# Eight fetched experts per chunk and a shared last tile, in place of all sixteen experts for every token

## The chip, the cores and the metric

One Trainium2 chip, one of its cores. The metric is device microseconds of that core for one execution; lower is better. The engines are named as in the profile: PE (TensorE), DVE (VectorE), ACT (ScalarE), POOL (GpSimd), SP (SyncE, which here only issues DMAs).

## What is computed

The input `x` is 128 sequences of 64 tokens with 128 features; `ctx_1024` has the same shape. Everything is float32. Four residual steps follow each other:

```python
x = x + L0_xattn(layernorm(x), ctx)      # 16 heads of 8
x = x + L0_ffn(layernorm(x))             # 8 experts each pick 8 tokens of a sequence and attend among them
x = x + L1_xattn(layernorm(x), ctx)      # self-attention, cross-attention, a 128-512-128 net, three layernorms
x = x + L1_ffn(layernorm(x))             # the expert layer that the change is about
```

The expert layer has 16 routed experts and 2 shared ones, each with three 128 x 128 matrices:

```python
scores = sigmoid(x @ router_w.T);  s = scores + bias
keep the 2 best of 4 groups of experts, then the 4 best experts of those by s
w = 2.5 * scores[chosen] / sum(scores[chosen])          # combine weights, 0 for the other 12
h, u = x @ gate_w[e], x @ up_w[e]                       # for every e
routed = sum over e of w[e] * ((silu(h) * u) @ down_w[e])
y = routed + shared experts (weight 1)
```

The bias spreads by 0.8 between the experts, while the scores lie between 0 and 1, so that some experts are chosen by nearly every token and some by hardly any.

## The kernel before

The 8192 tokens are 16 chunks of 512 (8 sequences). A chunk's features lie over the 128 partitions and its tokens along the free axis when it is multiplied (`zT`), or tokens over partitions in four groups of 128 when it is normalized. Chunks 0 to 15 first go through the first layer (loop at the end of `two_layers`, with `routed_attention` for two chunks at a time); the results go to DRAM (`x_mid`). Then each chunk goes through `decoder_block` and `expert_layer`.

Nothing is issued when the Python code runs. The class `Plan` records every operation and gives it a cost in us by the function `duration` (for PE, 0.86 for a 128x512 matmul; for SP, 0.4 for the issue of a DMA and 2.2 and more until it has landed). `Plan.run` then simulates five engines with these costs and writes the instructions in the order in which they would start, at most `WINDOW` = 5 chunks past the oldest unfinished one, each engine strictly in order. So every recorded operation has the same line in the profile, L364 (the call in `Plan.run`), and it is told apart by its tile. Buffers are named slots: `PLACES` says which tags share them. SP issues nearly all DMAs, in one queue of instructions, in order; a DMA whose buffer or data is not ready holds up all that stand behind it.

The expert layer before:

- Six loads bring all 18 experts' matrices to SBUF once (`wg`, `wu`, `wd`), after the first layer has let go of these places.
- `run(c, x)` normalizes the chunk (`normed`, `turned`: `zT`) and calls `route`, which computes the combine weights `w` with some 40 small DVE instructions, transposes them (`psc`), copies them on DVE (`comb`), writes them to DRAM (`comb_d`), and reads them back by eight DMAs of two experts each, every row spread over all 128 partitions (`all_w`, 512 KB each).
- Then a loop over 18 experts, each on all 512 tokens. PE does `gate` and `up`, ACT a tanh (`mo_g`), DVE two steps (`mo_g`, `mo_a`: silu times up), POOL a multiplication by `all_w[e]` (routed experts only), and PE adds `wd[e]` times that to the sum `py`.
- `py` is copied (`yT`), transposed (`pt`) and added to `x`, which goes out.

In PSUM `gate` and `up` share five banks with other matmuls; `mo_g` and `mo_a` have three buffers each.

In `Attention.run`, used three times per chunk, the keys are spread by head in four copies (`kx`): two by ACT, two by DVE; the queries (`q`) are scaled on DVE.

Of the kernel before, what the change touches and what calls it, by code (L numbers as in the profile page):

```python
# [17 lines left out]
F32 = mybir.dt.float32  # L18
I32 = mybir.dt.int32
AF = mybir.ActivationFunctionType  # L20
ALU = mybir.AluOpType
# [17 lines left out]
NG, TKG, TOPK = 4, 2, 4  # L39
EPG = E1 // NG  # L40
BEHIND = 100
EARLY = 6
# [22 lines left out]

C_M4, C_BM, C_RK, C_COS, C_SIN, C_TRI, C_R8, C_END = 0, 4, 132, 134, 198, 262, 278, 286


# [94 lines left out]
class Plan:  # L163
# [3 lines left out]
    def __init__(self, tc, window, prompt=(), pace=0, places=None):  # L167


        self.prompt, self.pace, self.places, self.after = prompt, pace, places or {}, set()  # L170
        self.behind = 0.0
        self.tc, self.nc, self.window = tc, tc.nc, window
        self.ops, self.chunk, self.group = [], 0, None
        self.free, self.turns, self.known = {}, {}, {}
        nc = tc.nc
        self.V, self.A, self.G, self.T, self.Y = (
            Recorder(self, e, n) for e, n in ((nc.vector, "V"), (nc.scalar, "A"), (nc.gpsimd, "G"), (nc.tensor, "T"), (nc.sync, "Y"))
        )
# [190 lines left out]


class Recorder:
    def __init__(self, plan, eng, name):
# [6 lines left out]
def duration(engine, method, out, args, kw):  # L379

    n = elements(out)
    if engine == "T":
        if method == "transpose":
            return 0.11, 0.3, (128, False)
        lhsT, rhs = kw["lhsT"], kw["rhs"]
        k, m = (lhsT.shadow if isinstance(lhsT, View) else lhsT).shape[:2]
        one = max(0.00084 * n, 0.00087 * max(m, 64))
        together = (4 if k <= 32 else 2 if k <= 64 else 1) * (2 if m <= 64 else 1)
        return 2 * one / together, 0.3, (min(k, 64) if k <= 32 else 128, m <= 64)
    if engine == "Y":  # L390
        return 0.4, 2.2 + n * out.shadow.shape[0] * 5.0e-6 * 4, None
# [20 lines left out]
    "r": ["r.0", "r.1", "lg.0", "lg.1"], "h0": ["rot.0"], "h1": ["rot.1"],  # L412
    "z4": ["hotT1.0"], "zT4": ["zr.0", "zr.1"], "yT": ["hotT0.0"], "comb": ["zTr.0"],
    "mo_g": ["y.0", "ra_v.0", "ra_v.1"], "mo_a": ["scT.0", "rsc.0", "rsc.1"],
    "all_w": ["trig.0", "xp.0", "wvo.0", "sw.0", "sw.1"],
    "wg": ["xg.0"], "wu": ["xg.1"], "wd": ["wqk.0"],
    "m2": ["m.0", "m.1", "m.2"], "py": ["m.3"],
# [3 lines left out]
def two_layers(ctx: ExitStack, tc: tile.TileContext, a: dict, out: bass.AP):  # L421
# [8 lines left out]
    make_identity(nc, ident)  # L430
    cst = const.tile([P, C_END], F32, name="cst")
    nc.sync.dma_start(out=cst, in_=a["consts"])
# [16 lines left out]

    ones = const.tile([P, S], F32, name="ones")  # L450
    nc.vector.memset(ones, 1.0)
# [3 lines left out]


    x_mid = [kept.tile([P, T, P], F32, name=f"xm{c}", tag=f"xm{c}") for c in range(NCH)]

# [44 lines left out]
    class Attention:  # L503
# [10 lines left out]
        def __init__(self, pl, sb, ps, n_v, n_kx):  # L514
            one = const
            self.pl, self.sb, self.ps, self.n_kx = pl, sb, ps, n_kx

            v_bd = [one.tile([P, NB, NP, 2 * V1], F32, name=f"v_bd{i}", tag=f"v_bd{i}") for i in range(n_v)]
            self.v_bd = [pl.held(t) for t in v_bd]
            for t in self.v_bd:  # L520
                pl.G.memset(t, 0.0)
                pl.G.memset(t[:S, :, :, HD : HD + 1], 1.0)
                pl.G.memset(t[S:, :, :, V1 + HD : V1 + HD + 1], 1.0)

            self.bk = {}
            for w in ("L0_xattn_", "L1_xattn_sa_", "L1_xattn_ca_"):
                self.bk[w] = one.tile([P, NR], F32, name=f"bk{len(self.bk)}", tag=f"bk{len(self.bk)}")
                nc.vector.tensor_scalar(self.bk[w], cst[:, C_M4 : C_M4 + NR], col[w + "bk"], None, ALU.mult)
            self.n = 0

        def run(self, c, zT, kvT, w, resid, dst, mask=None, role="", bank="m"):
# [10 lines left out]
            for h in range(NR):  # L542
                place = cst[:, C_M4 + h : C_M4 + h + 1]
                if h < 2:
                    A.activation(kx[:, h], psk, AF.Identity, bias=self.bk[w][:, h : h + 1], scale=place)
                else:
                    V.tensor_scalar(kx[:, h], psk, bk, place, ALU.add, ALU.mult)
            psq = m([P, CH], "psq")
            T_.matmul(psq, lhsT=wq, rhs=zT, start=True, stop=True)
            q = pl.new(sb, [P, CH], "q", self.n_kx, tag="q" + role)  # L550
            V.tensor_scalar(q, psq, bq, 1.0 / math.sqrt(HD), ALU.add, ALU.mult)

# [103 lines left out]
    def routed_attention(pl, sb, ps, dram):  # L656
# [8 lines left out]

        big = lambda name, tag, slots: pl.new(sb, [P, (E1 + 2) * P], name, slots, tag=tag)
        wqk = big("wqk", "wqk", 1)[:, : 2 * E0 * P].rearrange("p (e f) -> p e f", e=E0)
# [72 lines left out]
        def run(c, xs):  # L740
# [41 lines left out]
            for half in range(2):  # L782
# [48 lines left out]
                with pl.one():  # L831
                    for t in range(4):
                        T_.matmul(psa[:, t], lhsT=v[:, t], rhs=scT[:, t], start=True, stop=True)
                V.tensor_copy(xp[:, :, part].rearrange("p q e r -> p e q r"), psa.rearrange("p e (q r) -> p e q r", r=KT))

            for i, (x, gated) in enumerate(zip(xs, gates)):
# [72 lines left out]
    def expert_layer(pl, sb, dram, ps):  # L909
# [4 lines left out]
        pl.Y.dma_start(out=bias, in_=a["L1_ffn_bias"].unsqueeze(0).to_broadcast([P, E1]))  # L914
        wg, wu, wd = (pl.new(sb, [P, (E1 + 2) * P], n).rearrange("p (e f) -> p e f", f=P) for n in ("wg", "wu", "wd"))
        loads = [
            (wg, a["L1_ffn_gate_w"].rearrange("e d f -> d e f"), a["L1_ffn_sh_gate_w"].rearrange("d (u f) -> d u f", u=2)),
            (wu, a["L1_ffn_up_w"].rearrange("e d f -> d e f"), a["L1_ffn_sh_up_w"].rearrange("d (u f) -> d u f", u=2)),
            (wd, a["L1_ffn_down_w"].rearrange("e f d -> f e d"), a["L1_ffn_sh_down_w"].rearrange("(u f) d -> f u d", u=2)),
        ]  # L920
        last = []
        for w, routed, shared in loads:
            for part, src in ((w[:, :E1], routed), (w[:, E1:], shared)):
                pl.Y.dma_start(out=part, in_=src)
                last.append(pl.ops[-1])
        tri = cst[:, C_TRI : C_TRI + NG * NG].rearrange("p (i j) -> p i j", i=NG)
# [15 lines left out]

        def route(z):

# [55 lines left out]
            comb = pl.new(sb, [E1, CH], "comb", 1)  # L1000
            V.tensor_copy(comb, psc)

            flat = pl.new(dram, [E1, CH], "comb_d", 2)
            pl.Y.dma_start(out=flat, in_=comb)
            all_w = []
            for i in range(0, E1, 2):
                t = pl.new(sb, [P, 2, CH], "all_w")
                pl.Y.dma_start(out=t, in_=flat[i : i + 2].unsqueeze(0).to_broadcast([P, 2, CH]))
                all_w += [t[:, k] for k in range(2)]
            return all_w  # L1010

        def run(c, x):
            pl.after = set(last)
            zT = turned(pl, normed(pl, x, sb, role="4", n=1), sb, ps, "m2", role="4")
            pl.after = set()
            all_w = route(zT)
            py = pl.new(ps, [P, CH], "py")
            for e in range(E1 + 2):
                ph = pl.new(ps, [P, CH], "gate", tag="me")
                T_.matmul(ph, lhsT=wg[:, e], rhs=zT, start=True, stop=True)  # L1020
                pu = pl.new(ps, [P, CH], "up", tag="me")
                T_.matmul(pu, lhsT=wu[:, e], rhs=zT, start=True, stop=True)

# [3 lines left out]
                act = pl.new(sb, [P, CH], "mo_a", in_turn=True)  # L1027
                if e < E1:
                    V.tensor_tensor(act, g, pu, ALU.mult)
                    G.tensor_tensor(act, act, all_w[e], ALU.mult)  # L1030
                else:
                    V.scalar_tensor_tensor(act, g, 0.5, pu, ALU.mult, ALU.mult)
                T_.matmul(py, lhsT=wd[:, e], rhs=act, start=e == 0, stop=e == E1 + 1)
            yT = pl.new(sb, [P, CH], "yT", 1)
# [5 lines left out]
            V.tensor_tensor(x, x, pt, ALU.add)  # L1040
            pl.Y.dma_start(out=pl.held(out[c]), in_=x)
        return run

# [19 lines left out]
    for c in range(NCH):  # L1063
# [8 lines left out]
        attend.run(c, zT, cT, "L0_xattn_", x, x)  # L1072
        if c == 1:
            the_rest(pl)
            routed = routed_attention(pl, sb, ps, dram)
        if c % 2:
            routed(c - 1, xs[c - 1 :])

    for c in range(NCH):
        pl.chunk = NCH + c  # L1080
        pl.behind = BEHIND
        if c == 0:
            decoder = decoder_block(pl, sb, ps, attend)
            pl.after = marks[-1]
            experts = expert_layer(pl, sb, dram, ps)
            pl.after = set()
        x, cT = loaded(c, pl.held(x_mid[c]))
        pl.after = marks[EARLY if c < 2 else NCH // 2 - 1] if c <= WINDOW else set()
        decoder(c, x, cT)
        pl.after = set()  # L1090
        experts(c, x)
    pl.run()


def _constants():

    import numpy as np

    c = np.zeros((P, C_END), np.float32)
    p = np.arange(P)  # L1100
# [10 lines left out]
    i = np.arange(NG)  # L1111
    c[:, C_R8:] = np.arange(1, KT + 1)
    c[:, C_TRI:C_R8] = (i[None, :] < i[:, None]).astype(np.float32).reshape(-1)
# [41 lines left out]
```

## Time and profile before

| | |
|---|---|
| median of 3 runs | 2013.98 us (2008.09 to 2018.83) |
| the profiled execution | 2008.47 us |
| its span in the trace | 2006.5 us |
| mean granted clock of PE | 0.974 |
| first expert matmul of the second layer (`gate`, `py`) | from about 680 us |
| first `out` issued | 780.2 us |
| last `out` issued | 2003.5 us |
| chunk to chunk in the steady part (`sc` on POOL at 1006.88, 1097.33, 1187.78 us) | 90.45 us |
| longest waits of SP | for DVE's `comb` 605.7 us, for DVE's `x` 539.3 us |

The profile shows one execution. An engine's busy time counts the time in which at least one of its instructions ran. A float32 matmul is two instructions on PE; they are pipelined, and the end of each is modelled, so the time of one is read from the distance between starts. Groups give the count, the summed busy time, the mean of one, and then the idle time just before them with what ended it. SP's DMA issues appear as SPq.

### The profile page before, as it was taken

How to read it: one execution, taken by the hardware profiler on the slowest of the kernel's cores; microseconds unless marked ns; L12 is line 12 of the kernel's file. 1: busy time of each engine (PE TensorE's matmuls, PEld its weight loads, DVE VectorE, ACT ScalarE, POOL GpSimd, SP SyncE). 2: the span in 40 equal slices, each digit the busy share in tenths (PEclk: the TensorE clock that was granted, in tenths of full speed). 3: DMA queues.
4: the chain of work that ended last, by engine and by line, in shares of the span. 5: the costliest groups of instructions: out<-in, count | busy, mean ns of one | idle time of the engine just before them, and what ended most of it. 6: DMA issues, size and time to landing. Idle time of an engine off the chain costs nothing.

```text
span 2006.5 us, 41482 instructions
## 1 busy us (share of the span) xinstructions
PE 1876.2 (94%) x16032; PEld 1176.9 (59%) x16032; DVE 1490.5 (74%) x3694; ACT 999.9 (50%) x1987; POOL 1156.7 (58%) x1326
## 2 busy tenths in 40 slices
PE   5988889987888999999999999999999999999999
PEld 3776666776666655555564655555564656555444
DVE  4667767786886886878778786878778786777664
ACT  5866768676645535344443445344443444443322
POOL 5545656465565775565566565565566565555544
PEclk7988999998988999999999999999999999999999
DMA  4001111110220202111111203111111202111121
GB/s 132 14 20 40 46 46 35 48 41 23 76 79 9 78 12 103 51 54 54 51 59 46 94 12 103 54 51 54 51 56 49 89 16 91 54 38 59 70 92 54
DMA packets 64036, 110.62 MB, mean 55 GB/s; under 512 B 18016, under 2 KB 33120, under 8 KB 63840
## 3 DMA queue, kind: packets, MB, share of 16 engines
q1 hardware_dynamic: 63696, 107.91, 16.1%
q8 instruction: 126, 2.06, 0.4%
q14 instruction: 70, 0.57, 0.1%
q10 hardware_dynamic: 144, 0.07, 0.0%
HBM read 98.25 MB, written 9.70 MB: 54 GB/s over the span
## 4 chain that ended last, share of the span: by engine, by line
PE 49%; DVE 28%; POOL 10%; ACT 5%; issue 4%; SPq 2%; DMA 2%; DVEq 0%; POOLq 0%; ACTq 0%
PE pso L364 7%; PE up L364 7%; PE gate L364 7%; PE pst L364 7%; PE py L364 7%; POOL sc L364 4%; DVE mx L364 3%; DVE mo_a L364 3%; PE pss L364 2%; DVE kx L364 2%; DVE sc L364 2%; SPq L364 2%; POOL mo_a L364 2%; DVE mo_g L364 2%; DVE ln_st L364 1%
## 5 line engine op out<-in xcount | busy, mean ns | idle before, releaser
L364 POOL TENSOR_TENSOR sc<-sc,mx 128x512 f32<-128x512 f32 x384 | 397.4, 1059 | 233.1 <-DVE mx L364 228.2
L364 POOL TENSOR_TENSOR mo_a<-mo_a,all_w 128x512 f32<-128x512 f32 x256 | 325.1, 1272 | 257.4 <-DVE mo_a L364 256.9
L364 ACT ACTIVATE mo_g<-gate 128x512 f32<-128x512 f32 x288 | 171.4, 595 | 334.6 <-PE gate L364 331.6
L364 PE MATMUL up<-zT,wu 128*128 128x512 f32 x576 | 300.7, 604 | 4.8 <-DVE r L364 4.2
L364 ACT ACTIVATE e<-pst 128x512 f32<-128x512 f32 x384 | 217.9, 598 | 172.0 <-PE pst L364 153.6
L364 DVE SCALAR_TENSOR_TENSOR mo_g<-mo_g,gate 128x512 f32<-128x512 f32 x288 | 195.2, 679 | 143.6 <-ACT mo_g L364 141.7
L364 PE MATMUL gate<-zT,wg 128*128 128x512 f32 x576 | 298.8, 601 | 2.2 <-DVE q L364 0.8
L364 PE MATMUL py<-mo_a,wd 128*128 128x512 f32 x576 | 295.8, 596 | 0.7 <-DVE mo_a L364 0.7
L364 DVE TENSOR_REDUCE mx<-sc 128x8 f32<-128x512 f32 x384 | 245.1, 678 | 26.0 <-ACT sc L364 24.7
L364 PE MATMUL pst<-ident,sc 128*128 128x128 f32 x1536 | 229.0, 287 | 36.9 <-DVE mo_a L364 6.4
L364 PEld LDWEIGHTS pst<-ident,sc 128*128 128x128 f32 x1536 | 176.9, 145 | 109.8 <-POOL sc L364 45.5
L364 PEld LDWEIGHTS pso<-v_bd,e 128*64 128x64 f32 x6144 | 194.8, 139 | 53.7 <-issue 44.4
L364 PE MATMUL pso<-v_bd,e 128*64 128x18 f32 x6144 | 212.2, 213 | 0.5 <-ACT e L364 0.4
L364 DVE TENSOR_TENSOR mo_a<-mo_g,up 128x512 f32<-128x512 f32 x256 | 174.4, 681 | 29.9 <-PE up L364 22.4
L364 POOL TENSOR_TENSOR ln_rs<-ln_mv,powers 128x4 f32<-128x4 f32 x112 | 61.6, 551 | 181.3 <-DVE ln_mv L364 181.3
L364 PEld LDWEIGHTS up<-zT,wu 128*128 128x128 f32 x576 | 101.0, 190 | 107.7 <-issue 76.7
L364 PEld LDWEIGHTS py<-mo_a,wd 128*128 128x128 f32 x576 | 103.0, 191 | 100.2 <-issue 85.4
L364 POOL TENSOR_TENSOR r<-r,rows_t 128x512 f32<-128x512 f32 x112 | 142.2, 1274 | 29.0 <-PE tr_ps L364 20.7
L364 PEld LDWEIGHTS gate<-zT,wg 128*128 128x128 f32 x576 | 98.8, 191 | 98.8 <-issue 58.9
L364 PE MATMUL pss<-kx,q 32*64 32x256 f32 x3072 | 124.3, 396 | 3.5 <-DVE at L364 1.4
L364 ACT ACTIVATE r<-r,ln_off,ln_rs 128x128 f32<-128x128 f32 x192 | 81.0, 483 | 68.9 <-POOL ln_off L364 52.9
L364 ACT COPY v_bd<-psv 64x256 f32<-64x256 f32 x192 | 74.0, 385 | 72.8 <-PE psv L364 71.1
(163 smaller groups left out, 2935.6 us busy)
## 6 DMA issues: line engine op xcount, KB each, us to landing
all_w<-comb_d SPq DMA_DIRECT2D x128, 512.0 KB
cT<-in_ctxT SPq DMA_DIRECT2D x32, 256.0 KB
x<-in_x SPq DMA_DIRECT2D x16, 256.0 KB
psr<-rows_d SPq DMA_DIRECT2D x128, 32.0 KB
xm<-x SPq DMA_DIRECT2D x16, 256.0 KB
x<-xm SPq DMA_DIRECT2D x16, 256.0 KB
out<-x SPq DMA_DIRECT2D x16, 256.0 KB
k_raw<-in_mask_Bx1x1xS_if SPq DMA_DIRECT2D x32, 64.0 KB
```

What stands on the lines that cost most here:

```text
L364: made = getattr(eng, method)(*map(put, args), **{k: put(v) for k, v in kw.items()})
```

## The change

For each chunk the kernel counts how many tokens chose each expert, and takes the eight most chosen. Only these eight (and the two shared ones) are applied to the chunk's 512 tokens.

- **route** gets more steps. A matmul with ones counts the choices (`psn`), DVE adds a small term that breaks ties, and `max` and `max_index` give the eight numbers (`number`, in SBUF). SP reads each number into a register (`Sync.fetch`) and issues a DMA whose source address comes from it: first the expert's three matrices (`ew`, 196 KB, from a DRAM tensor that holds gate, up and down side by side), then the expert's row of `comb_d`, spread over the partitions (`all_w`, 256 KB). That is 16 such fetches per chunk.
- The weights of the experts that were not taken stay in `wl`. Tokens that have one are flagged (`fl`); two small matmuls (`psf`) and a scan on DVE give each a slot, counted on over all chunks (`base`). A one-hot matrix (`oh`, 128x512) and four matmuls (`left_ps`) put such tokens' normalized features, weights and position into their slots, and DVE adds that to `acc`.
- After the last chunk, **the_others** applies all 16 experts to the 128 slots of `acc`: four quarters of four experts, each with its own load of 786 KB, two times four matmuls, a tanh, two DVE steps, four down matmuls and four weighted sums (`yl`). POOL then adds the 128 rows of `yl` into `out` by an indirect DMA. Six one-element memsets on the last `x` buffers make it wait for the DMAs that write `out`.
- **general_path**: all five engines load the number of flagged tokens; if it is above 128, a loop that is written out (256 rounds) treats every chunk with every expert. Every chunk's `z` and overflow weights are written to DRAM for it (`z_over`, `w_over`).
- The six big weight loads go; two loads bring the shared experts (`shared`), after layer one's `gated`.
- In the second layer's attentions, the third `kx` copy and `q` go from DVE to ACT; `comb` is copied by ACT.
- The first layer's later weight loads get a later due time (`LATER`), and `ew` uses the slots of the first layer's matrices.
- The planner books a fetch at 0.8 us on SP and 3.2 us until it has landed.

The output gets 128 more rows in DRAM, for slots that stay empty; they are not returned.

In the order of instructions as written out, PE goes from 288 to 160 each of `gate`, `up` and `py` matmuls; DVE gets 21 more instructions per chunk; SP has 256 register loads and as many register operations that it did not have. SP's order in a middle chunk is four `ew`, `comb_d`, three `ew`, four `all_w`, one `ew`, four `all_w`.

```diff
+    def fetch(self, out, table, index, last, over=None):
+        e = self.nc.sync.value_load(index)
...
+        src = table[bass.ds(e, 1)]
+        src = src.rearrange("e p c -> (e p) c") if over is None else src.to_broadcast([over, src.shape[1]])
+        return self.nc.sync.dma_start(out=out, in_=src)
...
+    if method == "fetch":
+        return 0.8, 3.2, None
...
-                if h < 2:
+                if h < (3 if mask else 2):
                     A.activation(kx[:, h], psk, AF.Identity, bias=self.bk[w][:, h : h + 1], scale=place)
...
+            if mask:
+                A.activation(q, psq, AF.Identity, bias=self.bq[w], scale=1.0 / math.sqrt(HD))
...
-        wg, wu, wd = (pl.new(sb, [P, (E1 + 2) * P], n).rearrange("p (e f) -> p e f", f=P) for n in ("wg", "wu", "wd"))
...
+        shared = [pl.new(sb, [P, 3 * P], f"shared{u}") for u in range(2)]
...
-            V.tensor_copy(comb, psc)
+            A.copy(comb, psc)
+            V.tensor_scalar(ind, w, 0.0, None, ALU.is_gt)
+            T_.matmul(psn.rearrange("p t e -> p (t e)"), lhsT=ones, rhs=ind.rearrange("p t e -> p (t e)"), start=True, stop=True)
+            V.tensor_reduce(cnt, psn.rearrange("p t e -> p e t"), AX.X, ALU.add)
+            V.tensor_tensor(cnt, cnt, cst[:, C_TIE : C_TIE + E1], ALU.add)
+            V.max(out=most, in_=cnt)
+            V.max_index(out=number, in_max=most, in_values=cnt)
...
+            for h in range(2):
+                ew.append(pl.new(sb, [P, 2 * E0 * P], "ew", in_turn=True)[:, : 12 * P].rearrange("p (k c) -> p k c", k=4))
+                for k in range(4):
+                    pl.Y.fetch(ew[h][:, k], table=a["L1_ffn_w"], index=number[0:1, 4 * h + k : 4 * h + k + 1], last=E1 - 1)
+            for h in range(KD // 2):
                 t = pl.new(sb, [P, 2, CH], "all_w")
-                pl.Y.dma_start(out=t, in_=flat[i : i + 2].unsqueeze(0).to_broadcast([P, 2, CH]))
+                for k in range(2):
+                    pl.Y.fetch(t[:, k], table=flat, index=number[0:1, 2 * h + k : 2 * h + k + 1], last=E1 - 1, over=P)
...
+            V.tensor_tensor(wl, w, cnt.unsqueeze(1).to_broadcast([P, T, E1]), ALU.mult)
...
+            V.tensor_tensor(
+                oh, cst[:, C_SLOT : C_SLOT + SLOTS].unsqueeze(1).to_broadcast(dims), slot.unsqueeze(2).to_broadcast(dims), ALU.is_equal
+            )
+                for t in range(T):
+                    T_.matmul(psx, lhsT=oh[:, t], rhs=z4[:, t], start=t == 0, stop=t == T - 1)
+            V.tensor_tensor(acc, acc, psx, ALU.add)
...
+            pl.Y.dma_start(out=pl.held(w_over[c]), in_=wo)
+            pl.Y.dma_start(out=pl.held(z_over[c]), in_=z)
...
-            for e in range(E1 + 2):
+            experts = shared + [ew[k // 4][:, k % 4] for k in range(KD)]
+            for i, m in enumerate(experts):
...
+        def the_others(xs):
...
+            for q in range(E1 // 4):
+                m = pl.new(sb, [P, 2 * E0 * P], "ew", in_turn=True)[:, : 12 * P].rearrange("p (k c) -> p k c", k=4)
+                pl.Y.dma_start(out=m, in_=a["L1_ffn_w"][4 * q : 4 * q + 4].rearrange("e p c -> p e c"))
...
+            G.add_rows(pl.held(out), rows=yl, index=row_at)
...
+    def general_path(yl, count):
+        n = nc.values_load(count[0:1, 0:1], min_val=0, max_val=NCH * CH)
+        with tc.If(n > SLOTS):
...
-    out = nc.dram_tensor("out_0", (n_seq // NB, P, T, P), F32, kind="ExternalOutput").ap()
+    out = nc.dram_tensor("out_0", (n_seq * S + P, P), F32, kind="ExternalOutput").ap()
```

## The prediction

> **What bounds the kernel now.** I read the page first: busy shares, slices, then the chain that ended last.
>
> ```profile
> PE 1876.2 (94%) x16032; PEld 1176.9 (59%) x16032; DVE 1490.5 (74%) x3694; ACT 999.9 (50%) x1987; POOL 1156.7 (58%) x1326
> ...
> PE   5988889987888999999999999999999999999999
> ...
> PEclk7988999998988999999999999999999999999999
> ```
>
> TensorE is busy 94% of the span; from slice 14 (about 700 us) on it is full. The chain gives PE 49% and DVE 28%. The stretches show a steady state there. One chunk of the second layer takes 90.45 us (columns: length; PE, PEld, DVE, ACT, POOL busy; clock, DMA share, GB/s), against a stretch of the first layer:
>
> ```profile
> 500.00:600.00 100.00, 85.30 (x1094) 64.79 (x1092) 87.20 (x203) 53.17 (x108) 59.08 (x73) 0.95 0.26 78
> ...
> 1006.90:1097.35 90.45, 88.36 (x677) 51.12 (x676) 70.48 (x177) 39.81 (x78) 54.24 (x63) 1.00 0.17 58
> ```
>
> PE idles 2.1 of 90.45 us there: what leaves PE shortens the period until another engine is next. DVE is, at 70.5. The first row is the highest DVE share of any 100 us stretch: 87%, with PE down at 85%. I take 87% as about what DVE reaches in this program before PE waits for it.
>
> What one expert matmul costs is read from the timeline, not from the group's 601 ns, which overlaps its neighbour:
>
> ```profile
> 1966.64 1.02 PE L364 MATMUL py<-mo_a,wd 128*128 128x512 f32 x2
> 1967.50 1.02 PE L364 MATMUL up<-zT,wu 128*128 128x512 f32 x2
> 1968.36 1.02 PE L364 MATMUL gate<-zT,wg 128*128 128x512 f32 x2
> ```
>
> One every 0.858 us.
>
> **What is removed, per chunk.** 18 experts become 10 (2 shared, 8 fetched).
> - PE: 8 x 3 x 0.858 = 20.6 us.
> - DVE and POOL, from these rows:
>
> ```profile
> L364 POOL TENSOR_TENSOR mo_a<-mo_a,all_w 128x512 f32<-128x512 f32 x256 | 325.1, 1272 | 257.4 <-DVE mo_a L364 256.9
> L364 DVE SCALAR_TENSOR_TENSOR mo_g<-mo_g,gate 128x512 f32<-128x512 f32 x288 | 195.2, 679 | 143.6 <-ACT mo_g L364 141.7
> L364 DVE TENSOR_TENSOR mo_a<-mo_g,up 128x512 f32<-128x512 f32 x256 | 174.4, 681 | 29.9 <-PE up L364 22.4
> ```
>
> DVE loses 8 x (0.679 + 0.681) = 10.9, and what moves to ACT: comb 0.67, two of the kx at 0.80, two q at 0.74: 14.6 in all. POOL loses 10.2 (54.2 to 44.1). ACT loses 8 x 0.595 and takes five operations of 0.6 to 0.8: 39.8 to 38.5. Both stay off the bound.
>
> **What is added, per chunk.**
> - PE: psn and two psf matmuls at the r_psl row's 0.12 us an instruction (two each), four left_ps at 0.25: 1.8 us. PE work becomes 88.4 - 20.6 + 1.8 = 69.6.
> - DVE: 21 instructions in route: oh like any 128x512 (0.68), acc 0.3 (between the 128x64 and 128x256 rows), max_index 0.25 (load plus match rows), the rest 0.06 to 0.22 by size: 5.0. Nine read two SBUF tensors, and such rows come in two sizes:
>
> ```profile
> L364 DVE TENSOR_TENSOR g_gt<-g_gt,g_eq 128x64 f32<-128x64 f32 x16 | 16.6, 1037 | 1.6 <-POOL g_eq L364 0.3
> ...
> L364 DVE TENSOR_TENSOR w<-w,tot 128x64 f32<-128x64 f32 x16 | 3.6, 223 | 0.1
> ```
>
> The same shape is 0.8 us dearer where it meets a POOL operation. Nine such meetings would add 7.2, none 0; most two-tensor rows are near the low end, so I add 2. DVE work becomes 70.5 - 14.6 + 7 = 62.9 (60.9 to 68).
> - The period: PE at today's idle gives 71.7; DVE at 87.2% gives 62.9 / 0.872 = 72.1. Two engines that near their limits wait for each other, so I take 73. The bounds are 71.7 and 68 / 0.872 = 78.
>
> **The fetches.** After psn, DVE makes number (about 2 us); then SP runs, 16 times per chunk, a register load, a register operation, a wait and a DMA. SP had few such issues, and no load into a register is in this trace. The issue itself is 0.37 us (median of all_w). The load is one word from SBUF: at least a small engine operation (POOL's 0.20 us), at most a DMA round trip. That one is shown by what SP waits for comb_d, 26.7 us in 16 times:
>
> ```profile
> SPq L364 <- DMA comb_d<-comb: 26.7, 16, 3.4
> ```
>
> So with 0.1 each for register operation and wait a fetch holds SP for 0.8 to 2.2 us. I take 1.3, nearer the low end because one word without descriptors is nearer the small operation. Data lands 2.2 us after issue (1.67 plus 229 KB at the 375 GB/s of the all_w bursts). All 3.7 MB of a chunk need 9.8 us at that rate, less than 16 fetches take.
>
> Is that early enough? In the new order of instructions (chunk 8), with PE work priced as above and stretched to the period, py of the first fetched expert stands 18 us behind psn, gate of the eighth 27, its py 51. SP's order is four weights, comb_d, three weights, four all_w, a weight, four all_w. The first all_w, eighth in line, lands at 2 + 0.4 + 8x + 2.2 and is needed 1.6 us (POOL and hand-over) ahead of py, at 16.4: in time while x is at most 1.5. The eighth weight (12x + 4.6 against 27) allows 1.9, the last all_w 2.8. At 1.3 nothing is late but in the last chunks, where the order is tighter: 5 us in all. At 2.0 each chunk stalls by 4.2 us, at 2.9 by 12.4.
>
> Behind the first register load, which waits for DVE's number, stand on SP the previous chunk's out, w_over, cT, the mask and the x of five chunks on; SP's load per chunk is 16 x 1.3 + 4 = 25 us of 73, so these are late by some 10 us, and the next cross-attention's cT, needed first, is half a period away. The dummy write to out and the larger cst cost 0.4 us at the start; loads reordered there are worth a few us either way, taken as 0.
>
> A late fetch costs more than its wait. After an idle of 4.91 us this trace shows the clock down:
>
> ```profile
> 477.71 2.08 PE L364 MATMUL psk<-zT,mats 128*128 128x512 f32 x2 [4.91 <-DVE x L364]
> ...
> 480.00:490.00 10.00, 8.62 (x42) 5.50 (x42) 9.27 (x17) 4.79 (x10) 8.64 (x10) 0.63 0.01 2
> ```
>
> In those 10 us 8.62 busy us at 0.63 do the work of 5.4: some 4 us more per stall of this length. The Trainium skill (TensorE: Matmul & The Clock Gate, "Part 1") says the clock halves once PE has been idle and comes back after about 3.4 us of sustained work; the row agrees, and by that rule every stalled chunk pays it again.
>
> The Trainium skill (Runtime: NRT & Kernel Launch, "The ~15µs preamble/postamble breakdown") gives 1.3 us for register loads from HBM at launch; with the other terms that would be x = 1.9, and the sum below would be some 55 us more. No run here shows it yet.
>
> **The end.** Today 4.7 us lie behind the last py (2001.8 to 2006.5). After: the third quarter of the last tile's weights can load only when the last chunk's second four experts are done: 0.4 + 1.7 + 786 KB at 375 GB/s (2.1) = 4.2; its matmuls 2.7, tanh and two DVE steps 2.0, four 128x128 sums 1.1, hand-overs 0.5: 6.3. Then 0.3, the adding scatter by POOL (no row: a DMA's 2 us to five times that; I take 4), and the count's load on five engines and the branch (no row: 0 to 10; 3). That is 18, or 14 more. The Trainium skill (Runtime: NRT & Kernel Launch, "Instruction fetch mechanics") warns that a taken branch outside the fetched pages stalls; here one branch, once.
>
> **Sum.** 2006.5 + 16 x (73 - 90.45) + 14 + 5 = 1746 for the span; the run lies 2 us above its span (2008.47), so 1748. The median of the runs shown (2013.98) is 0.27% above that execution: 1753, rounded to 1755.
>
> **Rivals.**
> 1. *The fetch is dear* (x of 1.6 to 2.8): PE waits each chunk. At x = 2.0: 16 x (4.2 + 3) = 115, so about 1870. For: nothing shows the load's price. Against: 18 us of PE work stand in between.
> 2. *DVE becomes the bound* outright: period 78, 1835. For: the 1037 ns rows. Against: POOL is less busy than before.
> 3. *Slower:* one mechanism, the chain number, load, fetch, all_w, py. From x = 2.9 on each chunk waits 12.4 us and runs 4 us cold, 262 in all, which eats the gain of some 255; at 3.2 it is about 2080. For: SP is strictly in order and PE too. Against: it needs a word's load to cost 2.3 us, more than a whole DMA round trip here.
> 4. *The last tile overflows.* The router's arithmetic on the reference's inputs leaves 113 tokens outside their chunk's eight, under 128; a flip of 16 is unlikely. The branch would run 256 serial rounds of a 196 KB load and some 6 us of work, over 2 ms: above 4000.
>
> **Chances.** Forecast 0.62; rival 1 0.20; 2 0.08; 3 0.08; 4 0.02. Faster by over 0.5% (what a measurement of this kernel can tell from no change) 0.88, within 0.02, slower 0.10. Range: low, 16 x 1.3 less by a period of 71.7, a scatter and branch at their low ends (5 less), 20 for kinder first-layer ordering: 1710. High: x = 2.2, stalls of 5.8 + 3 per chunk, 140 more: 1895; this covers rivals 1 and 2 and leaves 0.10 above, less below.
>
> **What would show it.** Right: PE about 69.6 and DVE 61 to 65 us per period of about 73, clock 1.00; SP waiting for number rather than PE for all_w; register loads under 0.7 us. Wrong: gaps of PE at py or gate put down to POOL mo_a or a DMA of ew; a granted clock below 1 in the steady part; DVE above 90%; a last chunk followed by more than 30 us.

## The result, and the profile after

| | before | changed |
|---|---|---|
| median of 4 runs each | 2011.03 us | 1833.71 us (1818.98 to 1844.3) |
| ratio, with 95% interval | | 0.9108 [0.9037, 0.9179] |
| the profiled execution, its span | 2008.47, 2006.5 us | 1831.23, 1829.3 us |
| mean granted clock of PE | 0.974 | 0.948 |
| one chunk in the steady part | 90.45 us | 76.8 us |

The kernel is 8.9% faster. The forecast was 1755: the side and the range hold, the time is 79 us longer than said (a gain of 177 us where 259 were forecast). In the code as changed the call that issues every recorded operation is L371 (L364 before), and a fetch is L394 to L399. The page of the changed kernel, the lines that answer to those shown of before:

```profile
PE 1624.7 (89%) x15585; PEld 1098.8 (60%) x15585; DVE 1325.3 (72%) x3770; ACT 972.7 (53%) x1944; POOL 1002.5 (55%) x1199
...
PE   5979987998888899998989989898898999989787
...
PEclk8889999999998899999999999999999999999999
```

The busy time of every engine fell, and PE is no longer full from slice 14 on: there are 8s, and 7s at the end. The order now repeats every three chunks. Two such stretches (length; PE, PEld, DVE, ACT, POOL busy; clock, DMA share, GB/s):

```profile
927.64:1158.40 230.76, 215.02 (x1926) 135.94 (x1926) 174.62 (x535) 113.14 (x226) 133.57 (x159) 0.96 0.22 65
1158.40:1388.32 229.92, 211.55 (x1926) 133.44 (x1926) 175.56 (x535) 113.37 (x226) 133.62 (x159) 0.99 0.22 66
```

Divided by six chunks: period 76.8, PE busy 71.1, DVE 58.4 (76%). PE idles 5.7 us per chunk (2.1 before), and the clock is below 1 where it was 1.00. So neither PE nor DVE is full. The timeline shows what PE waits for: at `psc`, the transposing of the weights `w`, for DVE. The router's steps on DVE end just then; its small operations, with four larger ones of other steps between them, stand one behind the other from the first score (938.16) to `w` (949.0). PE's waits at `psc` are 21.4 of its 73.9 us of waiting between 720 and 1700 us, those at `psn` (the counting of the choices), right beside it, another 12.5.

```profile
949.15 1.01 PE L371 MATMUL psc<-ident,w 128*16 128x128 f32 x4 [4.96 <-DVE w L371]
```

Behind this wait the clock is down (a stretch of 5 us, same columns as above):

```profile
950.00:955.00 5.00, 5.00 (x10) 2.36 (x10) 3.44 (x21) 1.54 (x3) 1.22 (x2) 0.57 0.29 85
```

PE is busy all 5 us at 0.57, so 2.1 us of work are lost behind the 4.96 of waiting. Cut finer, the granted clock is 0.50 from 949.15 to 952.5, 0.65 from there to 955 and 1.00 in the next 5 us. The Trainium skill (TensorE: Matmul & The Clock Gate, "Part 1") gives half rate after an idle window of about 3.4 us until at least as long a stretch of work has passed; the half rate agrees, and here it lasted some 5 us of work.

### The profile page after: what moved, and what is told of

Read it like the earlier page. It is cut to its first block, busy times and chain, and to the rows that moved or that the text cites. A ratio compares the mean times of both kernels' runs of the same rounds, so it can differ in the third digit from the quotient of the medians.

```text
span 1829.3 us, 41640 instructions
## 1 busy us (share of the span) xinstructions
PE 1624.7 (89%) x15585; PEld 1098.8 (60%) x15585; DVE 1325.3 (72%) x3770; ACT 972.7 (53%) x1944; POOL 1002.5 (55%) x1199
## 3 DMA queue, kind: packets, MB, share of 16 engines
q1 hardware_dynamic: 86992, 104.40, 18.7%
## 4 chain that ended last, share of the span: by engine, by line
PE 46%; DVE 29%; ACT 9%; issue 5%; POOL 5%; DMA 3%; SPq 3%; DVEq 0%; POOLq 0%; ACTq 0%
PE pso L371 8%; PE pst L371 7%; PE py L371 5%; PE up L371 5%; DVE mx L371 4%; PE pss L371 4%; PE gate L371 3%; DVE sc L371 3%; SPq L371 3%; DVE mo_g L371 2%; DVE ln_st L371 2%; DVE mo_a L371 2%; POOL ln_rs L371 2%; PE psw L371 2%; ACT r L371 2%
## 5 line engine op out<-in xcount | busy, mean ns | idle before, releaser
L371 POOL TENSOR_TENSOR sc<-sc,mx 128x512 f32<-128x512 f32 x384 | 397.1, 1057 | 179.5 <-DVE mx L371 172.6
L371 ACT ACTIVATE e<-pst 128x512 f32<-128x512 f32 x384 | 217.0, 597 | 213.9 <-PE pst L371 178.8
L371 PE MATMUL pst<-ident,sc 128*128 128x128 f32 x1536 | 227.5, 288 | 51.7 <-DVE rot L371 17.6
L371 DVE TENSOR_REDUCE mx<-sc 128x8 f32<-128x512 f32 x384 | 245.6, 676 | 28.2 <-ACT sc L371 27.5
L371 PEld LDWEIGHTS pst<-ident,sc 128*128 128x128 f32 x1536 | 176.6, 146 | 110.3 <-issue 34.3
L371 PEld LDWEIGHTS pso<-v_bd,e 128*64 128x64 f32 x6144 | 200.1, 141 | 54.9 <-issue 29.4
L371 PE MATMUL pso<-v_bd,e 128*64 128x18 f32 x6144 | 217.6, 215 | 2.3 <-DVE sc L371 1.5
L371 POOL TENSOR_TENSOR r<-r,rows_t 128x512 f32<-128x512 f32 x112 | 142.2, 1271 | 132.7 <-PE tr_ps L371 108.9
L371 POOL TENSOR_TENSOR mo_a<-mo_a,all_w 128x512 f32<-128x512 f32 x128 | 163.0, 1287 | 92.1 <-DVE mo_a L371 90.0
L371 ACT ACTIVATE mo_g<-gate 128x512 f32<-128x512 f32 x160 | 93.8, 594 | 178.7 <-PE gate L371 155.2
L371 POOL TENSOR_TENSOR ln_rs<-ln_mv,powers 128x4 f32<-128x4 f32 x112 | 61.6, 550 | 206.0 <-DVE ln_mv L371 204.5
L371 PE MATMUL up<-zT,ew 128*128 128x512 f32 x256 | 131.5, 607 | 3.5 <-DVE mo_g L371 2.0
L371 PE MATMUL gate<-zT,ew 128*128 128x512 f32 x256 | 129.6, 606 | 3.1 <-ACT v_bd L371 2.2
L371 PE MATMUL py<-mo_a,ew 128*128 128x512 f32 x256 | 131.8, 601 | 0.0
L371 PE MATMUL pss<-kx,q 32*64 32x256 f32 x3072 | 121.4, 402 | 3.5 <-ACT wvT L371 2.6
L371 DVE SCALAR_TENSOR_TENSOR mo_g<-mo_g,gate 128x512 f32<-128x512 f32 x160 | 106.3, 680 | 22.4 <-ACT mo_g L371 22.2
L371 ACT ACTIVATE kx<-psk,bk,cst 128x512 f32<-128x512 f32 x128 | 95.1, 777 | 25.4 <-PE psk L371 25.1
L371 DVE TENSOR_TENSOR sc<-pss,qk_m 128x512 f32<-128x512 f32 x128 | 82.8, 682 | 32.5 <-PE pss L371 32.4
L371 DVE TENSOR_TENSOR mo_a<-mo_g,up 128x512 f32<-128x512 f32 x128 | 85.8, 681 | 26.7 <-PE up L371 18.8
L371 ACT ACTIVATE r<-r,ln_off,ln_rs 128x128 f32<-128x128 f32 x192 | 81.1, 484 | 42.3 <-POOL ln_off L371 25.7
L371 DVE TENSOR_TENSOR sc<-pss,k_m 128x512 f32<-128x512 f32 x128 | 82.4, 683 | 20.9 <-PE pss L371 20.8
L371 ACT ACTIVATE z<-x,ln_off,ln_rs 128x128 f32<-128x128 f32 x192 | 80.9, 488 | 25.6 <-POOL ln_off L371 10.8
```

Of the source, the lines that this page charges most:

```text
L371: made = getattr(eng, method)(*map(put, args), **{k: put(v) for k, v in kw.items()})
```

## The experiments

Four questions: are the fetches hidden, is DVE's load or the planner's pricing of DVE what PE waits for, what does the part for left tokens (those with a chosen expert outside their chunk's eight) cost, and why. Ratios are to the kernel before on the same chip; 0.0050 of ratio is 10 us. The changed kernel stands at 0.9108.

### 1. The fetch

Two kernels: the number loaded five times per fetch, and no number loaded at all (the places 0 to 7 are fetched, not the chosen experts).

```diff
-        e = self.nc.sync.value_load(index)
+        for k in range(5):
+            r = self.nc.sync.value_load(index)
+            e = r if e is None else e + r if k % 2 else e - r
```

> Each fetch loads its number five times (the register sum of the extra ones is zero), in the same order of instructions; SP needs about 2.0 us per fetch in place of 0.83. By the prediction's count (first all_w late by 8 x 2.0 + 4.6 - 16.4 = 4.2 us per chunk, and up to 3 us of cold clock) 70 to 115 us more: 1900 to 1950. If the fetches have far more room than that count says: 1825 to 1850. If they are already what PE waits for: each chunk later by 16 x 1.2 = 19 us, 2140.

Measured 1983.53 us, 0.9847 [0.9806, 0.9887]: 150 us slower than the changed kernel.

```diff
-        e = self.nc.sync.value_load(index)
...
-        src = table[bass.ds(e, 1)]
+        self.turn = getattr(self, "turn", -1) + 1
+        src = table[self.turn % 8 : self.turn % 8 + 1]
```

> Fetches from fixed places 0 to 7 without a register load; the same order otherwise. The output is not the reference's, since the eight fetched experts are not those chosen. The fetches then no longer wait for number and take 0.37 us each on SP. Theory A: the fetches were hidden, so 1815 to 1840 (no change). If the chain of number, load and fetch were on the path: 20 to 60 us less.

Measured 1827.93 us, 0.9063 [0.9015, 0.9111]: no change that can be told. The fetch costs the changed kernel nothing beyond the noise of some 10 us. Its price in the trace of the changed kernel is a register load of 0.27 us (columns: line, engine queue, operation, tile, count: least, median and greatest ns), and a fetch holds SP for 0.83 to 0.96 us (five issues within 4.17 us, two within 1.17):

```profile
L394 SPq TENSOR_LOAD <-number x256: 260/270/477, 687.0 to 1792.8; - x128
```

```profile
952.14 4.17 SPq L399 DMA_DIRECT2D ew<-in_L_ffn_w  x5
956.88 0.33 SPq L399 DMA_DIRECT2D all_w<-comb_d  x1
957.71 1.17 SPq L399 DMA_DIRECT2D ew<-in_L_ffn_w  x2
```

With five loads the same five issues take 9.31 us, 2.2 per fetch, and PE's waits (in us, times, longest) are the ones the prediction named for a dear fetch; neither stands among PE's longer waits in the changed kernel:

```profile
PE py L371 <- POOL mo_a L371: 51.5, 33, 3.6
PE gate L371 <- DMA ew<-in_L_ffn_w: 39.0, 17, 4.1
```

At x = 2.2 (us that a fetch holds SP, as in the prediction) the prediction's sum says 5.8 + 3 us per chunk, 141 in all; 150 came, and the two waits make 90.5 where the sum has 16 x 5.8 = 93. My expectation for this run (1900 to 1950) was too low because it took each extra load at too little. The sum's total holds, with some luck: it has the first `all_w` eighth in SP's order, while in two of three chunks of the trace it is sixth, where the sum would give a shorter wait.

### 2. DVE: its load and its price in the plan

My first theory (A) was that the plan books the router's small steps at 0.06 to 0.13 us, while those of 64 elements stand 0.22 to 0.26 us apart in the trace, so that PE meets `psc` too early. Booked as they are, booked still smaller, and all small DVE steps booked at 0.2 us:

```diff
+            if engine == "V":
+                t = max(t, self.least)          # least = 0.23 within route, 0 elsewhere
```

> The planner books each small DVE step of route at 0.07 to 0.13 us; the trace of the changed kernel shows about 0.23 from step to step in that chain. Here route's DVE steps are booked at no less than 0.23 us; no instruction is added or dropped. Theory A (PE, in order, stands before psc and psn until DVE's routing chain is done, because the planner puts them too early, and then runs cold): PE's idle for psc and psn in the steady part, 34 us in all, falls under 10, the clock rises from 0.95 towards 0.97, time 1775 to 1800. Rival B (DVE's load and its meetings with POOL set the period): DVE's work is the same, so 1820 to 1845. Rival C (any new order is worth 1% either way by luck): 1815 to 1850 with psc and psn waits not ordered by the booking.

```diff
+            if engine == "V":
+                t = min(t, self.least) if self.least else t     # least = 0.05 within route
```

> The counterpart: route's DVE steps are booked at no more than 0.05 us, so psc and psn stand still earlier in PE's order. Theory A: waits for psc and psn grow beyond 34 us, to 60 to 110, clock 0.93, time 1860 to 1920. Rival B: 1820 to 1845. Rival C: 1815 to 1850.

```diff
-        return 0.06 + n / 960 + (0.12 if ... else 0.0), 0.15, None
+        return max(0.2, 0.06 + n / 960) + (0.12 if ... else 0.0), 0.15, None
```

> Every DVE instruction is booked at no less than 0.2 us, in both layers, not only route's. Theory A: as in the run with route alone or better, 1765 to 1800, the first layer changing a little too. Rival B: 1820 to 1845.

Measured 1832.75 us, 0.9082 [0.9042, 0.9121]; 1862.27, 0.9243 [0.9204, 0.9282]; 1822.12, 0.9071 [0.9030, 0.9112]. A price too small by more costs 1.5%, so the price does matter; but the right one brings nothing that can be told from the changed kernel. PE's waiting between 720 and 1700 us is 69.7 us with the real price (73.9 without): the 21.4 at `psc` became 11.1 there, 9.1 behind `v_bd` at `psc` and 10.0 at `psv`. Theory A falls: the price chooses where PE waits, not whether.

Then the load: the third `kx` copy and `q` put back on DVE, and the other way round, these moves and that of `comb` alone in the kernel before.

```diff
-                if h < (3 if mask else 2):
+                if h < 2:
...
-            if mask:
-                A.activation(q, psq, AF.Identity, bias=self.bq[w], scale=1.0 / math.sqrt(HD))
```

> The third kx copy and q of the second layer's attentions go back to DVE (3.1 us per chunk more on DVE, 58.4 to 61.5 of 76.7). If DVE sets the period: 16 x 3.1 = 50 more, 1880. If PE's order does: 1820 to 1850.

> The kernel before with only the moves to ACT (third kx, q, comb). PE is full there and DVE 78% busy, so 1995 to 2015: no change.

Measured 1835.08 us, 0.9126 [0.9086, 0.9167]: no change, so more work on DVE costs the changed kernel nothing, and DVE is not its bound. In the kernel before, the moves alone give 1986.19, 0.9877 [0.9845, 0.9908]: 25 us, where I had expected none.

### 3. What the part for left tokens costs

```diff
@@ route
             all_w += [t[:, k] for k in range(2)]
+            return ew, all_w
@@ two_layers
-    yl, count = the_others(later[-6:])
-    general_path(yl.place(), count.place())
```

> Leaves out everything for the tokens outside the eight experts: flags, slots, one-hot, left_ps, acc, the last tile, the stores for the overflow and the branch (113 tokens miss an expert's share). Routing, counting and fetching stay. By the prediction's terms: 1.6 us of PE and 4 us of DVE per chunk and 14 us at the end: if PE's work is what counts, 26 + 14 = 40 less, 1780 to 1800; if DVE is what counts, 64 + 14 = 78 less, 1745 to 1765; if the order's waits are what counts, only the end: 1810 to 1825.

Measured 1697.72 us, 0.8439 [0.8408, 0.8470]: 136 us less than the changed kernel, where the prediction has 1.6 us of PE per chunk (its 1.8 without `psn`, which stays) and 14 at the end, 40 in all. Four chunks take:

```profile
974.81:1258.16 283.35, 271.36 (x2521) 169.88 (x2520) 222.64 (x644) 149.38 (x301) 178.53 (x212) 0.99 0.22 67
```

A period of 70.8 us, PE busy 67.8, and no wait at `psc`. Without the end alone:

```diff
-    yl, count = the_others(later[-6:])
-    general_path(yl.place(), count.place())
```

> Leaves out the last tile's sixteen experts, the adding of its rows and the branch (tokens outside their chunk's eight miss that share), but keeps all that each chunk does for them, the holding of z among it. The forecast's end of 14 us: 1815 to 1823, and what is left to the 1698 of the kernel without the whole part, some 120 us, belongs to the chunks. Rival: the end costs more than what lies behind the last py (its loads and buffers reach back into the last chunks): 1790 to 1805.

Measured 1814.2 us, 0.9038 [0.9008, 0.9069]: 14 us by the ratios, whose intervals overlap a little; the traces bear it out, since 3.2 us lie behind the last `out` here and 16.9 in the changed kernel. So the end is what it was said to be, and some 120 us lie in the chunks, where the part's matmuls take about 2 us each time, and where 3 us more of DVE work cost nothing (section 2). Something else that the part does costs the rest.

### 4. Why: the buffer of z

The timeline of the changed kernel over one chunk, cut to the steps from one writing of `z` to the next:

```profile
1005.80 1.18 PE L371 MATMUL left_ps<-z,oh 128*128 128x147 f32 x8
1007.31 1.63 ACT L371 ACTIVATE z<-x,ln_off,ln_rs 128x128 f32<-128x128 f32 x4
...
1010.87 1.06 PE L371 MATMUL r_psl<-rw,zT 128*128 128x16 f32 x8 [0.86 <-ACT zT L371]
...
1023.50 0.60 PE L371 MATMUL psc<-ident,w 128*16 128x128 f32 x4 [2.08 <-DVE w L371]
1024.80 0.33 PE L371 MATMUL psn<-ind,ones 128*128 128x64 f32 x2
...
1074.02 0.28 PE L371 MATMUL psf<-fl,cst 128*128 128x4 f32 x2
...
1082.75 1.18 PE L371 MATMUL left_ps<-z,oh 128*128 128x147 f32 x8
1083.96 1.65 ACT L371 ACTIVATE z<-x,ln_off,ln_rs 128x128 f32<-128x128 f32 x4 [0.54 <-PE left_ps L371]
```

`z` is written right behind a `left_ps`, at 931.11, 1007.31, 1083.96 and 1161.88: 76.2, 76.7 and 77.9 us apart, the period. The diff says why. Before, `z` was read by its transposes only. Now four `left_ps` matmuls read it as well, as the last step of the chunk's choosing, and `z4` has one place (`"z4": ["hotT1.0"]`), as it had before. The next chunk's `z`, its transposes, its router product and its choice cannot start before that (in what follows, the hold). And `left_ps` stands 55 to 62 us behind `psn` in the steady part: its chain has little behind it in its chunk, so the plan's rank puts it last (`fl` is made at 1027.6; `psf`, which reads it, comes at 1074). So router and experts of a chunk no longer lie beside those of the next as PE needs, and PE meets `psc` while `w` is being made. In the trace little of this is a wait of ACT for PE (`z` behind `left_ps`: 10.0 us in all), because the plan knows of the hold and orders everything around it.

The test: a second place, one that the first layer's `z` has left; nothing else is changed.

```diff
-    "z4": ["hotT1.0"], "oh": ["hot.0"], ...
+    "z4": ["hotT1.0", "z.0"], "oh": ["hot.0"], ...
```

> The normalized chunk z of the second layer gets a second buffer (a place that the first layer's z has left); nothing else is changed. Theory H (the hold): in the changed kernel the left_ps matmuls of a chunk come last of its steps and read z, so z of the next chunk, its router product and its choice start only after them (ACT's z starts within 0.6 us of the end of left_ps in each of the chunks looked at) and PE runs out of other work at psc. Then the idle time of PE between 720 and 1700 us falls from 74 us to 40 or less, the wait at psc goes, and the time falls by 40 to 80 us, to 1755 to 1795. Theory W (the work): the 136 us that went with the whole part for left tokens are its own matmuls, DVE steps and end. Then the second buffer moves the order and the time stays within 1% of the changed kernel's 1834 (1815 to 1850).

Measured 1751.65 us (1751.30 to 1772.74), 0.8753 [0.8695, 0.8811]: 82 us less than the changed kernel by the medians, 71 by the ratios; 40 to 80 had been expected. Page and a stretch of two chunks:

```profile
PE 1582.1 (90%) x15585; PEld 1070.3 (61%) x15585; DVE 1342.2 (77%) x3770; ACT 965.9 (55%) x1944; POOL 1000.4 (57%) x1199
...
PEclk9989999999998899999999999999999999999999
```

```profile
978.84:1125.27 146.43, 138.56 (x1287) 87.13 (x1285) 120.73 (x357) 74.65 (x150) 89.00 (x107) 1.00 0.23 69
```

Per chunk 73.2 us, PE 69.3, DVE 60.4, clock 1.00. PE has the same 15585 matmuls and is busy 42.6 us less: that is clock, since busy time times mean granted clock is the same, 1624.7 x 0.948 and 1582.1 x 0.973, both 1540. Its waiting between 720 and 1640 us is 47.6 us (68.9 in the changed kernel over the same stretch), with none at `psc`; that is above the 40 that I had set for the somewhat longer stretch to 1700. Theory H holds but for that number, theory W doesn't. Where the 80 us between the two profiled spans lie, by the times of `out` (first 767.77 and 749.34, eleventh 1537.06 and 1495.11, last 1812.39 and 1732.82), with PE busy and clock behind the length:

```profile
767.77:1537.06 769.29, 713.96 (x6446) 450.85 (x6446) 583.77 (x1781) 378.66 (x753) 446.60 (x531) 0.97 0.22 65
1537.06:1812.39 275.33, 243.56 (x1505) 142.81 (x1505) 187.65 (x635) 100.61 (x197) 119.90 (x134) 0.96 0.28 86
```

```profile
749.34:1495.11 745.77, 703.45 (x6609) 446.44 (x6610) 609.31 (x1801) 377.69 (x760) 450.88 (x538) 1.00 0.22 67
1495.11:1732.82 237.71, 227.93 (x1401) 129.96 (x1399) 176.15 (x573) 94.06 (x186) 116.67 (x128) 1.00 0.30 92
```

24 us lie in the ten chunks of the middle, and 38 in the last five: there PE idles 31.8 of 275 us against 9.8 of 238. The likely reason is that no later chunk's attention is left there to fill the hold. The 18 before the first `out` are not all the hold's: the kernel without the end, whose order on PE is the changed kernel's up to 1590 us, had its first `out` at 755.77, so 12 of them vary from execution to execution.

With two places `z` still follows a `left_ps` in every period, now that of two chunks before (985.10 and 986.31, 1058.05 and 1059.33). Is there more in it? Two more kernels: the left part ranked 30 us earlier with one place for `z`, and with three.

```diff
+            pl.behind -= 30.0
             V.tensor_scalar(cnt, cnt, most[:, KD - 1 : KD], None, ALU.is_lt)
...
             V.tensor_tensor(acc, acc, psx, ALU.add)
+            pl.behind += 30.0
```

> One buffer for z as in the changed kernel, the same operations; only the planner's rank of the left tokens' steps (from the comparison with the eighth count to the addition into acc) is put 30 us earlier, so that left_ps stands some 51 rows of PE's order behind psn instead of some 155. Theory H (z is held until left_ps, and left_ps comes last): the hold is short, the waits at psc go and the time falls as with two buffers, to 1735 to 1775. Rival L (the second buffer helped because it moved the order, or by its place, and not by ending the hold): 1810 to 1850. Rival U (urgent small DVE steps push DVE's large ones back): 1780 to 1810.

The second has the same two lines and:

```diff
-    "z4": ["hotT1.0"], "oh": ["hot.0"], ...
+    "z4": ["hotT1.0", "z.0", "z.1"], "oh": ["hot.0"], ...
```

> Three buffers for z and the left tokens' steps early. With two buffers z was still written right behind a left_ps (that of two chunks before, at 986.31 and 1059.33 us), so some hold was left. If the hold is all that is lost beside the part's own work and end: 1698 of the kernel without the part, plus 20 of the end, plus 16 times 2 of own PE work: 1735 to 1750. If two buffers had already ended it, no change to the run with two: 1745 to 1760. Rival: more freedom of order brings no gain or a loss, 1760 and above.

Measured 1790.08 us, 0.8897 [0.8851, 0.8944], and 1768.7, 0.8789 [0.8744, 0.8835]. The first ends the hold 21 us behind `psn` instead of 58 (psn 956.50, left_ps 977.15) without a second place and gains 42 us by the ratios, so rival L (1810 to 1850) falls. It does not reach the two places (theory H had 1735 to 1775), and its time lies in rival U's span. Its waits between 720 and 1640 us are 50.9 us, most of them for large DVE steps (`r` at `up`, `mo_g` at `psv`, `zT` at `psq`), which is what rival U says; that the early small steps cause them was not tried by itself. The second lies in the span of its last rival, and by the ratios can't be told from two places alone: nothing more was found in the hold.

The same two stretches as above, from the first `out` to the eleventh and from there to the last, tell more. First one place, early, then three places, early:

```profile
763.92:1521.68 757.76, 716.16 (x6421) 444.88 (x6420) 615.81 (x1786) 374.01 (x754) 446.34 (x535) 0.98 0.22 66
1521.68:1762.06 240.38, 230.90 (x1459) 132.66 (x1457) 179.94 (x558) 95.76 (x187) 118.54 (x133) 0.99 0.30 90
```

```profile
767.66:1507.50 739.84, 698.80 (x6455) 442.46 (x6454) 598.28 (x1792) 372.34 (x755) 446.78 (x534) 1.00 0.23 68
1507.50:1746.64 239.14, 230.00 (x1459) 132.69 (x1457) 180.66 (x558) 95.81 (x187) 119.33 (x133) 0.99 0.29 91
```

The early `left_ps` brings nearly as much as a second place in the last five chunks (240.4 us against 275.3 and 237.7), but only half as much in the middle (757.8 against 769.3 and 745.8). More places shorten the middle at either ranking, by 23.5 and by 17.9 us, so there the places count whatever the order. Three places lose to two ahead of the first `out` (767.66 and 749.34), a stretch of which 12 us varied between two executions above. Two places stay the best measured of the kernels that compute everything, some 4% under the changed kernel.

## Why the prediction was right in side and short in size

Its terms beside what the traces show, per chunk where not said otherwise:

| term | forecast | changed | two places for z |
|---|---|---|---|
| PE busy | 69.6 | 71.1 | 69.3 |
| PE idle | 3.4 | 5.7 | 3.9 |
| DVE busy | 62.9 (60.9 to 68) | 58.4 | 60.4 |
| ACT, POOL busy | 38.5, 44.1 | 37.8, 44.5 | 37.3, 44.5 |
| period | 73 | 76.8 | 73.2 |
| a fetch on SP | 1.3 (0.8 to 2.2) | 0.83 to 0.96 | |
| behind the last py | 18 | 19 | 18.7 |
| span | 1746 | 1829.3 | 1749.4 |

- **What is removed** was right. PE's own work per chunk is 69.3 where the clock is 1.00; the 1.8 us more in the changed kernel are clock (215.02 x 0.96 and 211.55 x 0.99 us over six chunks are 69.3 each).
- **DVE's work** came out below the range's low end of 60.9 (58.4; 60.4 with two places). The row that I feared shrank, and so did another:

```profile
L371 DVE TENSOR_TENSOR g_gt<-g_gt,g_eq 128x64 f32<-128x64 f32 x16 | 10.4, 648 | 0.0
...
L371 DVE TENSOR_TENSOR mk<-mk,off 128x64 f32<-128x64 f32 x16 | 5.6, 351 | 0.5
```

  1037 and 999 ns before. In the kernel before, 12 of the 16 steps `mk` overlap an operation of POOL and take 1.26 us on average; in the changed kernel 4 do. The others take 0.225 us in both. That speaks against rival 2 (DVE as the bound), and so does the run with more work on DVE: that its 1835 is nearly the measured time is chance.
- **The fetches**: hidden, as said, at less than the price that I took, with no stall at the end to show for the 5 us put down there. The Trainium skill's 1.3 us for register loads at launch (Runtime: NRT & Kernel Launch, "The ~15µs preamble/postamble breakdown") is not this load's price: the row says 0.27, near the 200 ns per register of the same page ("Instruction fetch mechanics"). The bound of x = 1.5 was not reached, and the run at 2.2 bears out the sum for the stall, though the order that it was read from holds for one chunk in three. The "some 55 us" at x = 1.9 leave out the 3 us of cold clock that the other sums count; with them it is about 100. Rivals 1 and 3 didn't come, by the price of a load, not by another mechanism; rival 4 didn't either.
- **The end** was right within 1 us in its total, and the kernel without it gives 14. Its 4 and 3 us for the scatter and the branch had no row behind them; from the issue of the scatter (1824.3) to the end of the span 5.0 us pass. The last `py` of the kernel before ends at 2001.4, not 2001.8.
- **The step that failed is the period**: "PE at today's idle gives 71.7; DVE at 87.2% gives 62.9 / 0.872 = 72.1. Two engines that near their limits wait for each other, so I take 73." The bounds were 71.7 and 78. It asks for the work of two engines and forgets the buffers. The change gives `z` a reader some 58 us behind `psn`, and `z` has one place, so a loop runs through the chunks, z, router, choice, left_ps, next z. In the plan's order this loop takes 76.8 us, though some 46 of them are no work but the stretch in which the plan leaves the part for left tokens aside (`fl` done at 1027.8, `psf` at 1074.0); with a second place the period is 73.2. The same hold costs 38 us in the last five chunks, which the sum of 16 equal periods priced as if they were like the middle. Nothing in the rivals covers it: they ask for a late transfer, a full engine or an overflow. The prediction held `left_ps` at 0.25 us a matmul, a right price (1.18 us for four); what it read was not asked. The step could be seen beforehand in the list of places, where `z4` has one, and in the order: in the trace `left_ps` stands only 12 to 16 groups of PE's matmuls ahead of the next chunk's `psn`.
- **The signs**: SP waits for `number` (113.2 us in 7 waits), register loads are under 0.7 us and DVE is under 90%, as listed for a right forecast. The list named "a granted clock below 1 in the steady part" as a sign of the wrong, and PE's gaps at `py` or `gate`. The first came, the second did not: the gaps are at `psc`, ahead of the choice and not behind the fetch.

With the second place the forecast is met: ratio 0.8753 [0.8695, 0.8811] against 1755 / 2013.98 = 0.871. Part of that is luck. The chunks behind the first `out` save 16.0 us each in place of 17.45, 22 us less than said over 15 of them; the first `out` comes 31 us earlier (780.2 and 749.34), 13 more than a chunk's saving, where the forecast had 0 for the first layer; and the 5 us for late fetches didn't come.

What stays open: from two places (0.8753) to the kernel without the part (0.8439) there are 63 us. The end is 14, the periods (73.2 and 70.8) give 16 x 2.4 = 38; the other 11 are within the two intervals and not assigned. And why the moves to ACT give 25 us in the kernel before while their undoing costs the changed kernel nothing was not tried; that the changed kernel's loop covers it is only argued.

## What to carry to other kernels

When a change gives a tile one more reader, ask where in the order that reader stands, how many places the tile has, and who wants the next one: work that is almost free (1.2 us of matmuls) can hold a buffer for most of a period, and the loop through that buffer can set the time though no engine is full. In a trace such a loop shows as the same pair, last read and next write, back to back in every period, with an interval equal to the period; it need not show as a wait, where a plan has ordered the rest around it. The pair alone proves nothing: it stands in the trace with two places too, where the period is 3.6 us shorter. What tells is a run with one more place. An order that a planner makes hides a wrong price and a missing place alike: change one of them alone and see whether the waits go or only move.

## What the runs showed of the hardware

- A load of one word from SBUF into an SP register takes 0.27 us (260 to 477 ns in 256 times); with the register operation and the issue a fetched DMA holds SP for 0.83 to 0.96 us.
- One idle stretch of 4.96 us of PE is followed by 5 us at a granted clock of 0.57 (950 to 955 us). Between the changed kernel and the one with two places the same matmuls differ by 42.6 us of busy time, about as much as the waiting itself differs in (204.6 and 167.3 us of span without PE: 37.3).
- A two-tensor DVE step of 128x64 took 0.225 us (`mk`) clear of POOL, and 1.26 us on average where it overlapped an operation of POOL (12 of 16 in the kernel before). `g_gt`, of the same shape, fell from 1037 to 648 ns in the changed kernel.
